# Layer 0 of a two-layer macaron block: attention work handed out one portion per score, FFN chains due later, and one FFN product moved to GpSimd

## The chip, the cores and the metric

One core of one Trainium2 chip runs the whole program in one launch. The metric is the device time of one execution in microseconds (us). The profile shows one execution: five engines with queues of their own (TensorE = PE for matmuls, PEld for its weight loads; VectorE = DVE; ScalarE = ACT; GpSimd = POOL; SyncE = SP, which here only issues DMAs). Each engine works through its own list of instructions strictly in order. That list is fixed when the program is built: a scheduler inside the tile framework takes the instructions in the order in which Python emits them as their priority, and places on each engine the first one that its own timing model holds ready. So the Python order is a wish, and the built order is what runs.

## The reference, cut to what matters

Sixteen sequences of 512 tokens with 128 features go through two layers. Layer 0 is FFN, attention, FFN:

```python
x = x + 0.5 * _L0_ffn_ref(_layernorm(x), w_gate, w_up, w_down)
x = x + _L0_attn_ref(_layernorm(x), W_qkv, b_qkv, W_out, b_out, rel_emb_k, rel_emb_v)
x = x + 0.5 * _L0_ffn_ref(_layernorm(x), w_gate, w_up, w_down)
# _L0_ffn_ref: every operand of a product is first quantised to FP4 in blocks of 16
gate = fp4_linear(x, w_gate); y = fp4_linear(x, w_up)
h = jax.nn.silu(gate) * y                     # 352 features
return fp4_linear(h, w_down)
# _L0_attn_ref: 16 heads of 8 features, relative positions clipped to +-64
score = einsum('bhqd,bhkd->bhqk', q, k) + einsum('bhqd,qkd->bhqk', q, pe_k)
attn = jax.nn.softmax(score, axis=-1)
ctx = einsum('bhqk,bhkd->bhqd', attn, v) + einsum('bhqk,qkd->bhqd', attn, pe_v)
```

Layer 1 (a mixture of experts, a linear attention, and the mixture again) is not touched by the change.

## The kernel before

**Units.** The attention of layer 0 is cut into 32 units: sequence b = 0..15 times half = 0, 1 (256 queries each). One unit needs 32 score tiles of 128 keys x 512 (four key tiles `kt` times eight query blocks `bb`), and it needs them twice. `maxima` computes each tile and VectorE reduces it to column maxima (line 341, tile `mx`); at the unit's end the maxima go through a transpose on TensorE (line 349), become a row `mn`, and are written to DRAM and back into a row of the query operand `BD`. `main` computes the tiles again, now with the maximum subtracted by the matmul, and ScalarE takes the exponential into `PT` (line 369). A score tile is four matmuls (line 263), and twelve where the block lies near the diagonal (the band: eight more, line 267). All score tiles of both kinds share three PSUM buffers (`sps`).

**Averages and band part.** After the eight tiles of one `kt`, `main` emits the 16 matmuls that average V (into `av`, two PSUM banks), and where a half-band is complete, two runs of matmuls for the relative values (into `rps`, one bank) and four ScalarE copies of it into `RV`. `run` (lines 270 to 274) chains the matmuls of one run. `PT` has three buffers. At the end of the unit `RV` goes to DRAM (`RD`) and back as `cr`, and ScalarE copies `av` to `cx`.

**Chains.** Around this run generators whose steps are emitted between the scores: `head` (the first FFN of a sequence's half), `prep` (layer norm, queries and keys, and the DMAs that write them to the DRAM tensors QS, QM and KSd), `prepV`, `fin` (adds `cr` to `cx` on VectorE, normalises, projects) and `tail` (the second FFN, then the store of x, line 486). `interleave` gives each generator a number of steps n and a stretch from f to t in units of time, and always advances the one whose next step is due first. `main` of unit u is due from u to u+1 with 59 steps; the stream of `maxima` runs from 0 to 32 and is 14 steps ahead.

**Loads.** In the middle of each unit's maxima `loads` brings in the operands of the unit after it: KS (keys, eight DMAs, once per sequence), BD (four, line 329) and TQ (four, line 330). `head` calls `xload` first, which loads the sequence's x into one of five buffers (line 475). All of these are issued from SP's queue.

**FFN.** `FFN.half` treats 256 tokens: layer norm, quantisation (`quant_steps`: VectorE, the last two steps on GpSimd, lines 79 and 81; tiles `q_y` and `q_M`, two buffers each), for each of two groups of 128 tokens the gate (lines 121 to 123) and the product with 'up' (lines 125 and 126), the quantisation of h, and the product with 'down'.

Of the kernel before, what the change touches and what calls it, by code (L numbers as in the profile page):

```python
# [8 lines left out]
F32 = mybir.dt.float32  # L9
# [3 lines left out]
AF = mybir.ActivationFunctionType  # L13
ALU = mybir.AluOpType
# [3 lines left out]
I = 352  # L18
# [65 lines left out]
class FFN:  # L84
# [22 lines left out]
    def half(f, xb, half, wk, pp):  # L107

        s=f.s; nc=s.nc
        xh=xb[:,2*half:2*half+2,:]  # L110
        xn=wk.tile([128,2,128],F32,name="f_x")
        yield from s.ln_steps(xh,xn,wk,2)
        for xq in s.quant_steps(xn.rearrange("p a b -> p (a b)"),wk,128,16,"xq"): yield
        ps=pp.tile([128,512],F32,name="mps")
        for j in range(2): nc.tensor.transpose(ps[:,j*128:(j+1)*128],xq[:,j*128:(j+1)*128],s.ident)
        xqT=wk.tile([128,256],F32,name="f_x"); nc.scalar.copy(xqT,ps[:,:256]); yield
        h=wk.tile([128,2,I],F32,name="f_h")
        for j in range(2):
            t=h[:,j,:]
            g=pp.tile([128,512],F32,name="mps")  # L120
            nc.tensor.matmul(g[:,:I],xqT[:,j*128:(j+1)*128],f.wguT[:,0,:],start=True,stop=True)
            nc.scalar.activation(t,g[:,:I],AF.Tanh,scale=0.5)
            nc.vector.scalar_tensor_tensor(t,t,1.0,g[:,:I],ALU.add,ALU.mult); yield
            u=pp.tile([128,512],F32,name="mps")
            nc.tensor.matmul(u[:,:I],xqT[:,j*128:(j+1)*128],f.wguT[:,1,:],start=True,stop=True)
            nc.vector.scalar_tensor_tensor(t,u[:,:I],0.5,t,ALU.mult,ALU.mult); yield
        for hq in s.quant_steps(h.rearrange("p a b -> p (a b)"),wk,128,44,"hq"): yield
        hq=hq.rearrange("p (a b) -> p a b",a=2)
        for j in range(2):
            ps=pp.tile([128,512],F32,name="mps")  # L130
            for c in range(3):
                P=min(128,I-c*128)
                nc.tensor.transpose(ps[:P,c*128:(c+1)*128],hq[:,j,c*128:c*128+P],s.ident)
            hT=wk.tile([128,3,128],F32,name="hT",bufs=1)
            nc.scalar.copy(hT[:,0:2,:],ps[:,:256])
            nc.scalar.copy(hT[:96,2,:],ps[:96,256:384])  # L136
            for c in range(3):
                P=min(128,I-c*128)
                nc.tensor.matmul(ps[:,384:512],hT[:P,c,:],f.wdT[:P,c,:],start=(c==0),stop=(c==2),skip_group_check=True)  # L139
            nc.vector.scalar_tensor_tensor(xh[:,j,:],ps[:,384:512],0.5,xh[:,j,:],ALU.mult,ALU.add); yield  # L140
# [5 lines left out]
class Attn0:  # L146
# [103 lines left out]
    @staticmethod  # L250
    def vers(kt,half):

        return 1 if kt*128+192<half*256+256 else 0
# [12 lines left out]
                w0=kt*128-blk*32-x+a.OFF  # L266
                nc.tensor.matmul(out[:,x*64:x*64+64],a.ET[:,w0:w0+128],TQ[:,:,b*32+4*x:b*32+4*x+4],start=False,stop=(x==7),skip_group_check=True)  # L267

    xnT={}; pend={}; last=None
    def run(a, mms):  # L270

        r=a.nc.tensor.matmul(*mms[0][0],**mms[0][1])
# [85 lines left out]
    def main(a, b, half, X, wk, big, pS, pA, pM):  # L358
        s=a.s; nc=a.nc; i=b%2
        u=(2*b+half)%3; BD=a.BD[u]; TQ=a.TQ[u]; KS=a.KS[b%2]; V=a.V[b%2]; RD=a.RD[half]; cr=a.cr[0]  # L360
        av=[pA.tile([128,512],F32,name=f"av{z}") for z in range(2)]
        RV=wk.tile([128,4,4,4,16],F32,name="RV")
        PT=[None]*4
        for kt in range(4):
            pt=big.tile([128,16,256],F32,name="PT"); PT[kt]=pt
            for bb in range(8):
                ps=pS.tile([128,512],F32,name="sps")
                a.scores(ps,kt,half,bb,BD,TQ,KS)
                nc.scalar.activation(pt[:,:,bb*32:bb*32+32].rearrange("p h (x j) -> p x h j",j=4),ps.rearrange("p (x h j) -> p x h j",x=8,j=4),AF.Exp)  # L369
                yield  # L370
            vs=a.vers(kt,half)
            mms=[]
            for z in range(4):
                for cg in range(4):
                    h=z*4+cg
                    o=av[z//2][cg*32:cg*32+32,(z%2)*256:(z%2)*256+256]
                    fs=(kt==0 and z%2==0)
                    mms.append(((o,V[:,2*kt-1+vs,h*9:h*9+32],pt[:,h,:]),dict(start=fs,stop=(kt==3),skip_group_check=True,tile_position=(0,cg*32))))
            a.run(mms)
            for _ in range(4): yield  # L380
            for hb in range(2):
                bl=range(hb*4,hb*4+4)
                ks=[k for k in range(4) if any(a.inband(k,half*8+x) for x in bl)]
                if max(ks)!=kt: continue
                rps=pA.tile([128,512],F32,name="rps")
                first=[True]*4
                mms=[]
                for b0 in bl[::2]:
                    ok=[(bb,k) for k in reversed(ks) for bb in (b0+1,b0) if a.inband(k,half*8+bb)]
                    for n,(bb,k) in enumerate(ok):  # L390
                        blk=half*8+bb
                        for x in range(8):
                            cg=x%4; col=(bb-hb*4)*128+(x//4)*64
                            v0=(blk*32-k*128+a.UO)//8
                            mms.append(((rps[cg*32:cg*32+32,col:col+64],a.TV[a.vers(k,half)][:,x,v0-8*a.vers(k,half):v0-8*a.vers(k,half)+4,:].rearrange("p v d -> p (v d)"),
                                PT[k][:,:,bb*32+4*x:bb*32+4*x+4]),
                                dict(start=first[cg],stop=(k==min(q for p,q in ok if p==bb)),skip_group_check=True,tile_position=(0,cg*32))))
                            first[cg]=False
                    a.run(mms); mms=[]
                    yield  # L400
                    yield
                for c in range(4):
                    nc.scalar.copy(RV[:,:,c,:,hb*8:hb*8+8].rearrange("p j z a -> p a z j"),rps.rearrange("p (a z c j) -> p c a z j",a=8,z=4,j=4)[:,c])
                yield

        nc.sync.dma_start(RD[:,:4*8*1024].rearrange("x (r f) -> x r f",f=1024),RV)
        for c in range(4):
            src=bass.AP(tensor=RD.tensor,offset=RD.offset+c*64,ap=[[1024,8],[8*1024+256,16],[1,64]])
            nc.sync.dma_start(cr[c*32:c*32+8].rearrange("p (xj f) -> p xj f",f=64),src)
        cx=wk.tile([128,4,256],F32,name="cx")  # L410
        for zz in range(2):
            nc.scalar.copy(cx[:,2*zz:2*zz+2,:].rearrange("p z (b j x) -> p (z b) x j",j=4,x=8),av[zz].rearrange("p (y x j) -> p y x j",x=8,j=4))
        a.pend[b,half]=cx,cr
        yield

    def fin(a, b, half, X, wk, pM):

# [28 lines left out]
def interleave(*gens):  # L446

    live=[[g,n,0,f,t] for g,n,f,t in (q if len(q)==4 else (*q,0,1) for q in gens)]
    while live:
        k=min(live,key=lambda r:r[3]+(r[4]-r[3])*r[2]/r[1])  # L450
        try: next(k[0]); k[2]+=1
        except StopIteration: live.remove(k)
# [4 lines left out]
def layer0(tc, s, w, src, dst, nb=16):  # L457
    nc=tc.nc
    tok=lambda x,b: x[b].rearrange("(t p) d -> p t d",p=128)
    P="L0_attn_"; names=["W_qkv","b_qkv","W_out","b_out","rel_emb_k","rel_emb_v"]  # L460
    with ExitStack() as c:
# [9 lines left out]
        X={}  # L471
# [7 lines left out]
        def prep(b):  # L479
            if b<nb: yield from A.prep(b,X[b],wk,pM)  # L480
        def prepV(b):
            if b<nb: yield from A.prepV(b,pM)
# [7 lines left out]
        def loads(u):  # L490
            if u<2*nb:
                if u%2==0: A.loadK(u//2)
                A.load(u//2,u%2)
# [6 lines left out]
        def part(n):  # L500
            for _ in range(n):
                if next(st,0)==0: return
                yield
        pl,hl=2,3
        W=dict(part=0,V=(.6,.7),fin=(.45,.9),prep=(0,.7),tail=1.0,head=(-.1,1))
        with tc.tile_pool(name="wp",bufs=1) as wp:
            for b in range(3): xload(b)
            F=FFN(s,w["L0_ffn_w_gate"],w["L0_ffn_w_up"],w["L0_ffn_w_down"],wp,pF)
# [3 lines left out]
            def run(g):  # L512
                for _ in g: pass
            run(prep(0)); run(prepV(0)); loads(0); run(mxs(0,0))
            FFN1.pre(s,wp,[pA.tile([128,512],F32,name=f"av{z}") for z in range(2)]+[pA.tile([128,512],F32,name="rps")],w)
        big=c.enter_context(tc.tile_pool(name="big",bufs=3))
        loads(1); ffn2(head,1); run(prep(1)); run(part(14)); ffn2(head,2)
        S=[(part(99999),33*2*nb,W['part'],2*nb+W['part'])]
        for b in range(nb):
            for h in range(2):  # L520
                u=2*b+h
                def at(g,n,f,t): S.append((g,n,u+f,u+t))
                at(A.main(b,h,X,wk,big,pS,pA,pM),59,0,1)
                fn,tl=(W['fin'],W['tail']) if u<2*nb-2 else ((.3,.5),.6)
                at(A.fin(b,h,X,wk,pM),5,1+fn[0],1+fn[1])
                at(tail(b,h),21,1+fn[1]+.001,1+fn[1]+tl)
                if b+hl<nb: at(head(b+hl,h),21,*W['head'])
                if h==0 and b+pl<nb: at(prep(b+pl),11,*W['prep'])
                if h==1 and b+1<nb: at(prepV(b+1),1,*W['V'])
        interleave(*S)  # L530


# [249 lines left out]
class Attn1:  # L782
# [38 lines left out]
    X={}  # L821
# [216 lines left out]
```

## Time and profile before

| what | value |
|---|---|
| time, median of 3 runs | 3639.21 us (3634.64 to 3644.63) |
| the profiled execution's own time | 3633.94 us |
| its span | 3632.2 us |
| busy over the span | PE 78%, DVE 67%, ACT 47%, POOL 23% |
| first and last exponential of layer 0 (line 369) | start 175.5 us, 1974.5 us |
| 422 to 1692 us (22 units, 11 sequences): PE busy | 1126.22 of 1270 us |
| the same stretch: DVE, ACT, POOL busy | 1013.48, 647.68, 306.91 us |
| the same stretch: granted clock of PE | 0.98 |

The units between 422 and 1692 us repeat each other in pairs, one pair per sequence, so one of them can be read as a sample of all. In that stretch TensorE is busy most and idle 143.8 us, so what it waits for there is what sets the time of layer 0. Idle time of the other engines costs nothing unless TensorE waits for them.

### The profile page before, as it was taken

Reading aid. Unit: us, or ns where it says so; the run is one execution under the profiler, and the core shown is the slowest. Engines: PE = TensorE matmul, PEld = TensorE weight load, DVE = VectorE, ACT = ScalarE, POOL = GpSimd, SP = SyncE. Lnnn points to the kernel's source line nnn. Section 1 sums busy time; section 2 is a strip of 40 time slices with the busy share of each in tenths; the row PEclk is TensorE's granted clock in tenths of the full one; section 3 lists DMA queues with packets and bytes.
Section 4 is the critical chain, followed back from the end, with each engine's and each line's share of the span. In section 5 each row is a group of like instructions: output and inputs, shape, how many; then the busy total and the mean of one; then the engine's idle time right before and its main releaser. Section 6 shows DMA issues by size and latency. Waiting matters only on the chain. (4 is left out here: it accounts for less than half of the span.)

```text
span 3632.2 us, 95259 instructions
## 1 busy us (share of the span) xinstructions
PE 2825.0 (78%) x40077; PEld 2032.3 (56%) x40077; DVE 2444.9 (67%) x6508; ACT 1693.8 (47%) x3391; POOL 838.9 (23%) x789
## 2 busy tenths in 40 slices
PE   5578989889898889888896388873788888878570
PEld 3357777667676677666775244431565555555230
DVE  5568788777887788877773467774546655655356
ACT  3145555545455454545554155533455454445242
POOL 4122222222222222222110222212112211111226
PEclk8799999999999999999998599886899989989785
DMA  3232222321223222222210111104312222121401
GB/s 105 54 91 71 57 53 59 81 63 52 65 65 77 64 50 58 76 74 62 53 33 19 32 33 36 36 33 123 90 54 73 59 63 56 36 62 36 126 17 46
DMA packets 290159, 217.23 MB, mean 60 GB/s; under 512 B 77402, under 2 KB 257476, under 8 KB 289604
## 3 DMA queue, kind: packets, MB, share of 16 engines
q1 hardware_dynamic: 284468, 207.72, 21.6%
q8 instruction: 315, 5.16, 0.6%
q10 hardware_dynamic: 5264, 3.43, 0.4%
q14 instruction: 112, 0.92, 0.1%
HBM read 110.28 MB, written 100.78 MB: 58 GB/s over the span
## 5 line engine op out<-in xcount | busy, mean ns | idle before, releaser
L341 DVE TRANSPOSE_TENSOR_REDUCE mx<-sps 128x16 f32<-128x512 f32 x1024 | 702.5, 701 | 261.7 <-PE sps L263 137.2
L263 PE MATMUL sps<-a_BD,a_KS 128*128 128x128 f16 x8192 | 736.4, 222 | 136.2 <-DVE mx L341 65.6
L369 ACT ACTIVATE PT<-sps 128x512 f32<-128x512 f32 x1024 | 576.4, 599 | 433.8 <-PE sps L267 238.1
L263 PEld LDWEIGHTS <-a_KS 128*128 128x128 f16 x8192 | 546.1, 98 | 296.4 <-issue 260.0
L59 POOL TENSOR_TENSOR ln_rs<-ln_ve,negh 128x4 f32<-128x4 f32 (+1 forms) x192 | 176.9, 930 | 855.1 <-DVE ln_ve L58 760.6
L267 PE MATMUL sps<-a_TQ,a_ET 128*128 128x64 f16 x7168 | 370.3, 195 | 0.0
L721 DVE SCALAR_TENSOR_TENSOR moe<-mps,oh,moe 128x128 f32<-128x128 f32 x896 | 289.8, 341 | 110.7 <-PE mps L719 96.5
L79 POOL TENSOR_TENSOR q_M<-q_y,q_M 128x704 f32<-128x704 f32 (+2 forms) x129 | 157.0, 1218 | 784.6 <-DVE q_y L78 658.6
L719 PE MATMUL mps<-f_W,T 128*128 128x512 f32 x512 | 297.1, 701 | 24.8 <-DVE moe L721 20.0
L267 PEld LDWEIGHTS <-a_ET 128*128 128x128 f16 x7168 | 311.2, 99 | 2.3 <-issue 1.9
L274 PE MATMUL av<-PT,a_V 128*32 128x256 f32 x3840 | 251.9, 387 | 0.0
L894 DVE TENSOR_TENSOR a_at<-pp,a_cm 128x1024 f32<-128x1024 f32 x128 | 154.3, 1214 | 79.6 <-PE pp L892 78.6
L892 PE MATMUL pp<-a_F 64*128 64x128 f32 x2048 | 169.8, 306 | 41.4 <-DVE a_at L894 30.2
L892 PEld LDWEIGHTS pp<-a_F 64*128 64x128 f32 x2048 | 143.3, 206 | 93.0 <-DVE a_at L894 36.9
L719 PEld LDWEIGHTS mps<-f_W,T 128*128 128x128 f32 x512 | 102.7, 222 | 125.0 <-issue 75.3
L274 PEld LDWEIGHTS av<-PT,a_V 128*32 128x32 f32 x3840 | 121.4, 111 | 68.7 <-issue 5.0
L874 ACT ACTIVATE a_F<-pp 128x1024 f32<-128x1024 f32 x128 | 127.0, 1025 | 46.8 <-PE pp L872 40.5
L62 ACT ACTIVATE xn<-xn,ln_mr,ln_rs 128x128 f32<-128x128 f32 x256 | 103.6, 481 | 95.5 <-DVE ln_mr L60 75.2
L274 PE MATMUL rps<-PT,a_TV 128*32 128x64 f32 x6912 | 134.5, 222 | 4.6 <-issue 4.4
L139 PE MATMUL mps<-wdT,hT 128*128 128x128 f32 (+1 forms) x768 | 126.9, 301 | 5.6 <-ACT hT L136 4.0
L673 ACT COPY f_PT<-St 32x512 f32<-32x512 f32 x128 | 78.7, 615 | 106.0 <-DVE St L672 99.9
L872 PE MATMUL pp<-a_QK,a_PK 128*128 128x512 f16 x256 | 82.7, 413 | 54.4 <-DMA a_QK<-a1d 26.6
(342 smaller groups left out, 5330.2 us busy)
## 6 DMA issues: line engine op xcount, KB each, us to landing
QM<-a_HM SPq DMA_DIRECT2D x180, 128.0 KB
a_TQ<-QM SPq DMA_DIRECT2D x120, 192.0 KB
RD<-RV SPq DMA_DIRECT2D x32, 512.0 KB
a_KS<-KSd SPq DMA_DIRECT2D x128, 96.0 KB
a_QK<-a1d SPq DMA_DIRECT2D x128, 96.0 KB
xn<-X SPq DMA_DIRECT2D x32, 256.0 KB
a1d<-a_hi SPq DMA_DIRECT2D x64, 128.0 KB
a_BD<-QS SPq DMA_DIRECT2D x128, 58.0 KB
```

What stands on the lines that cost most here:

```text
L59: nc.gpsimd.tensor_tensor(rs,ve,s.negh[:,:n],ALU.pow); yield
L79: nc.gpsimd.tensor_tensor(M[:P],y[:P],M[:P],ALU.subtract)
L263: nc.tensor.matmul(o4[:,g],KS[:,sd,g*512+kt*128:g*512+(kt+1)*128],BD[:,g,:,b*32:b*32+32].rearrange("p h (x j) -> p x h j",j=4),start=(g==0 ...
L267: nc.tensor.matmul(out[:,x*64:x*64+64],a.ET[:,w0:w0+128],TQ[:,:,b*32+4*x:b*32+4*x+4],start=False,stop=(x==7),skip_group_check=True)
L274: for p,q in mms[1:]: a.nc.tensor.matmul(*p,**q)
L341: with a.s.tc.high_priority(): r=nc.vector.tensor_reduce(mx[:,kt,:,bb],ps.rearrange("p (i c) -> p i c",c=32),axis=AX.X,op=ALU.max,apply_tr ...
L369: nc.scalar.activation(pt[:,:,bb*32:bb*32+32].rearrange("p h (x j) -> p x h j",j=4),ps.rearrange("p (x h j) -> p x h j",x=8,j=4),AF.Exp)
L719: nc.tensor.matmul(ps,yT[:,j*128:(j+1)*128],a.W[:,e2*4:e2*4+4,:],start=True,stop=True)
L721: nc.vector.scalar_tensor_tensor(moe[:,j,:],ps[:,e*128:(e+1)*128],oh[:,j,e2*4+e:e2*4+e+1],moe[:,j,:],ALU.mult,ALU.add)
L874: nc.scalar.activation(f,ps,AF.Relu)
L892: nc.tensor.matmul(ps[:,hh,bs],f[hh*64:hh*64+64,1,bs],f[hh*64:hh*64+64,0,bs],start=True,stop=True)
L894: nc.vector.tensor_tensor(k,ps.rearrange("p h (b q) -> p (h b) q",b=4),a.cm.unsqueeze(1).to_broadcast([128,8,128]),ALU.mult)
```

## The change

**Portions.** `main` no longer emits averages and band part itself. It appends them as closures to a list `a.todo`: one for the 16 averaging matmuls of a `kt` (`avrun`), one for each half of a half-band (`rvrun`), one for the four copies (`rvcopy`), and one for the unit's end (the write of `RD`, the reads of `cr`, the copies of `av`). After each score of `main` one closure is taken from the list and run. What is left at a unit's end is run after the scores of the next; `rest` empties the list after the last. `main` now has 32 steps where it had 59.

**Due times.** The prologue no longer calls `ffn2(head,2)`; `head` is called for the sequence two ahead instead of three (`hl` 3 to 2) and is due from -1.15 to -0.05 instead of -0.1 to 1, that is from 2b-5.15 instead of 2b-6.1 for half 0 of sequence b. `prep` is due from 1.0 to 1.9 instead of 0 to 0.7, `fin` from 0.6 to 1.0 instead of 0.45 to 0.9, and `tail` follows `fin` as before. `loads` stays where it was.

**The product with 'up'.** VectorE's instruction at line 126 (0.5 times the PSUM tile u, times t) becomes a ScalarE copy of u, scaled by 0.5, into a `q_y` buffer, and a GpSimd multiplication of t by it.

```diff
-            nc.vector.scalar_tensor_tensor(t,u[:,:I],0.5,t,ALU.mult,ALU.mult); yield
+            v=wk.tile([128,704],F32,name="q_y")[:,:I]; nc.scalar.activation(v,u[:,:I],AF.Copy,scale=0.5); nc.gpsimd.tensor_tensor(t,t,v,ALU.mult); yield
...
-        av=[pA.tile([128,512],F32,name=f"av{z}") for z in range(2)]
-        RV=wk.tile([128,4,4,4,16],F32,name="RV")
-        PT=[None]*4
+        PT=[None]*4; T={}; vers=a.vers
+        def avrun(kt):
+            if kt==0: T["av"]=[pA.tile([128,512],F32,name=f"av{z}") for z in range(2)]
...
+            a.run(mms)
+        def rvrun(hb, b0, ks):
+            if b0%4==0: T["rps"]=pA.tile([128,512],F32,name="rps"); T["first"]=[True]*4
...
+            a.run(mms)
+        def rvcopy(hb):
+            if hb==0: T["RV"]=wk.tile([128,4,4,4,16],F32,name="RV")
+            for c in range(4):
+                nc.scalar.copy(T["RV"][:,:,c,:,hb*8:hb*8+8].rearrange("p j z a -> p a z j"),T["rps"].rearrange("p (a z c j) -> p c a z j",a=8,z=4,j=4)[:,c])
+        def end():
...
         for kt in range(4):
             pt=big.tile([128,16,256],F32,name="PT"); PT[kt]=pt
             for bb in range(8):
                 ps=pS.tile([128,512],F32,name="sps")
                 a.scores(ps,kt,half,bb,BD,TQ,KS)
                 nc.scalar.activation(pt[:,:,bb*32:bb*32+32].rearrange("p h (x j) -> p x h j",j=4),ps.rearrange("p (x h j) -> p x h j",x=8,j=4),AF.Exp)
+                if a.todo: a.todo.pop(0)()
                 yield
-            vs=a.vers(kt,half)
-            mms=[]
...
-            a.run(mms)
-            for _ in range(4): yield
+            a.todo.append(lambda kt=kt: avrun(kt))
             for hb in range(2):
                 bl=range(hb*4,hb*4+4)
                 ks=[k for k in range(4) if any(a.inband(k,half*8+x) for x in bl)]
                 if max(ks)!=kt: continue
...
-                    a.run(mms); mms=[]
-                    yield
-                    yield
...
+                a.todo+=[lambda hb=hb,b0=b0,ks=ks: rvrun(hb,b0,ks) for b0 in bl[::2]]+[lambda hb=hb: rvcopy(hb)]
+            if kt==3: a.todo.append(end)
+    def rest(a):
+        while a.todo: a.todo.pop(0)(); yield
...
-        pl,hl=2,3
-        W=dict(part=0,V=(.6,.7),fin=(.45,.9),prep=(0,.7),tail=1.0,head=(-.1,1))
+        pl,hl=2,2
+        W=dict(part=0,V=(.6,.7),fin=(.6,1.0),prep=(1.0,1.9),tail=1.0,head=(-1.15,-.05))
...
-        loads(1); ffn2(head,1); run(prep(1)); run(part(14)); ffn2(head,2)
+        loads(1); ffn2(head,1); run(prep(1)); run(part(14))
...
-                def at(g,n,f,t): S.append((g,n,u+f,u+t))
-                at(A.main(b,h,X,wk,big,pS,pA,pM),59,0,1)
+                def at(g,n,f,t): S.append((g,n,max(u+f,0),max(u+t,.5)))
+                at(A.main(b,h,X,wk,big,pS,pA,pM),32,0,1)
...
+        S.append((A.rest(),8,2*nb,2*nb+.15))
         interleave(*S)
```

More of the change, by code (lines that the diff above doesn't have):

```diff
@@ L267, in scores @@
                 nc.tensor.matmul(out[:,x*64:x*64+64],a.ET[:,w0:w0+128],TQ[:,:,b*32+4*x:b*32+4*x+4],start=False,stop=(x==7),skip_group_check=True)
-    xnT={}; pend={}; last=None
+    xnT={}; pend={}; last=None; todo=[]
     def run(a, mms):
@@ L360, in main @@
         u=(2*b+half)%3; BD=a.BD[u]; TQ=a.TQ[u]; KS=a.KS[b%2]; V=a.V[b%2]; RD=a.RD[half]; cr=a.cr[0]
-        av=[pA.tile([128,512],F32,name=f"av{z}") for z in range(2)]
-        RV=wk.tile([128,4,4,4,16],F32,name="RV")
-        PT=[None]*4
+        PT=[None]*4; T={}; vers=a.vers
+        def avrun(kt):
+            if kt==0: T["av"]=[pA.tile([128,512],F32,name=f"av{z}") for z in range(2)]
+            vs=vers(kt,half)
+            mms=[]
+            for z in range(4):
+                for cg in range(4):
+                    h=z*4+cg
+                    o=T["av"][z//2][cg*32:cg*32+32,(z%2)*256:(z%2)*256+256]
+                    fs=(kt==0 and z%2==0)
+                    mms.append(((o,V[:,2*kt-1+vs,h*9:h*9+32],PT[kt][:,h,:]),dict(start=fs,stop=(kt==3),skip_group_check=True,tile_position=(0,cg*32))))
+            a.run(mms)
@@ new lines, in rvrun @@
+        def rvrun(hb, b0, ks):
+            if b0%4==0: T["rps"]=pA.tile([128,512],F32,name="rps"); T["first"]=[True]*4
+            rps=T["rps"]; first=T["first"]
+            mms=[]
+            ok=[(bb,k) for k in reversed(ks) for bb in (b0+1,b0) if a.inband(k,half*8+bb)]
+            for bb,k in ok:
+                blk=half*8+bb
+                for x in range(8):
+                    cg=x%4; col=(bb-hb*4)*128+(x//4)*64
+                    v0=(blk*32-k*128+a.UO)//8-8*vers(k,half)
+                    mms.append(((rps[cg*32:cg*32+32,col:col+64],a.TV[vers(k,half)][:,x,v0:v0+4,:].rearrange("p v d -> p (v d)"),
+                        PT[k][:,:,bb*32+4*x:bb*32+4*x+4]),
+                        dict(start=first[cg],stop=(k==min(q for p,q in ok if p==bb)),skip_group_check=True,tile_position=(0,cg*32))))
+                    first[cg]=False
+            a.run(mms)
@@ new lines, in rvcopy @@
+        def rvcopy(hb):
[3 more added lines that the diff above has]
+        def end():
+            nc.sync.dma_start(RD[:,:4*8*1024].rearrange("x (r f) -> x r f",f=1024),T["RV"])
+            for c in range(4):
+                src=bass.AP(tensor=RD.tensor,offset=RD.offset+c*64,ap=[[1024,8],[8*1024+256,16],[1,64]])
+                nc.sync.dma_start(cr[c*32:c*32+8].rearrange("p (xj f) -> p xj f",f=64),src)
+            cx=wk.tile([128,4,256],F32,name="cx")
+            for zz in range(2):
+                nc.scalar.copy(cx[:,2*zz:2*zz+2,:].rearrange("p z (b j x) -> p (z b) x j",j=4,x=8),T["av"][zz].rearrange("p (y x j) -> p y x j",x=8,j=4))
+            a.pend[b,half]=cx,cr
@@ L369, in main @@
                 nc.scalar.activation(pt[:,:,bb*32:bb*32+32].rearrange("p h (x j) -> p x h j",j=4),ps.rearrange("p (x h j) -> p x h j",x=8,j=4),AF.Exp)
+                if a.todo: a.todo.pop(0)()
                 yield
-            vs=a.vers(kt,half)
-            mms=[]
[L373 to L378, printed above, removed]
-            a.run(mms)
-            for _ in range(4): yield
+            a.todo.append(lambda kt=kt: avrun(kt))
             for hb in range(2):
@@ L384, in main @@
                 if max(ks)!=kt: continue
[L385 to L398, printed above, removed]
-                    a.run(mms); mms=[]
-                    yield
-                    yield
[L402 to L414, printed above, removed]
+                a.todo+=[lambda hb=hb,b0=b0,ks=ks: rvrun(hb,b0,ks) for b0 in bl[::2]]+[lambda hb=hb: rvcopy(hb)]
+            if kt==3: a.todo.append(end)
+    def rest(a):
+        while a.todo: a.todo.pop(0)(); yield
     def fin(a, b, half, X, wk, pM):
```

## The prediction, made before the changed kernel ran

> **What bounds the kernel.** I read first the busy times by window: between 422 and 1692 us (22 units, 11 sequences) TensorE is busy 1126 of 1270 us, VectorE 1013, ScalarE 648, GpSimd 307. Of an average unit of 57.7 us TensorE idles 6.5, so the question is what ends that idle time. Second, TensorE's waits there (engine, tile and line <- releaser: total us, times, longest):
>
> ```profile
> PE sps L263 <- DVE mx L341: 40.1, 45, 3.9
> PE sps L263 <- ACT PT L369: 21.6, 56, 0.8
> PE mps L437 <- DVE a_V L321: 19.2, 11, 1.8
> PE mps L440 <- ACT cn L438: 11.4, 9, 1.8
> PE sps L349 <- DVE hq_sc L71: 9.9, 11, 0.9
> PE sps L349 <- DVE mk L347: 5.2, 11, 0.5
> ```
>
> The first row means that scores wait for a score buffer which VectorE has not yet reduced. Why is VectorE late? Third view, VectorE's own waits:
>
> ```profile
> DVE ln_st L55 <- DMA x<-in_L_attn_x_dram: 41.1, 10, 5.2
> ```
>
> Once per sequence VectorE stands still for a load of x. Fourth, the timelines of SP, VectorE and TensorE around one such wait (start, us, instruction, [idle before <- releaser]):
>
> ```profile
> 873.37 0.39 SPq L486 DMA_DIRECT2D X<-x  x1
> 876.73 0.39 SPq L475 DMA_DIRECT2D x<-in_L_attn_x_dram  x1
> 877.21 1.68 SPq L315 DMA_DIRECT2D a_KS<-KSd  x4
> 878.93 0.26 SPq L329 DMA_DIRECT2D a_BD<-QS  x1
> ...
> 890.76 3.52 SPq L330 DMA_DIRECT2D a_TQ<-QM  x1
> 894.37 0.72 SPq L406 DMA_DIRECT2D RD<-RV  x1
> ```
> ```profile
> 879.93 1.07 DVE L55 BATCH_NORM_STATS2 ln_st<-x 128x6 f32<-128x128 f32 x5 [4.11 <-DMA x<-in_L_attn_x_dram]
> ```
> ```profile
> 882.54 0.39 PE L263 MATMUL sps<-a_BD,a_KS 128*128 128x128 f16 x4 [2.85 <-DVE mx L341]
> ```
>
> The tail's store frees the x buffer, SP issues the load, 3.2 us later (876.73 to 879.93) VectorE goes on, and the scores lose 4.11 - 1.26 = 2.85 us: the buffers in hand cover 1.26 us and no more. That difference is 1.26 to 1.28 in all eleven pairs of such waits; the ten TensorE gaps from 532 to 1573 us sum to 28.5 us, 2.87 each with the one at 415 us.
>
> **The change, part by part.** Fifth view: the built order of both kernels (what stands behind what on each engine; no times). Sums are for the whole layer, with 14 sequences and 28 units of this kind (28/22 of the stretch).
>
> (a) *The load of x*, moved by head's new due time. Eleven x loads (sequences 5 to 15) need a buffer that a tail frees. Before, SP's order is store, x load, rest of KS, eight BD and TQ loads, RD write. After: one KS, store, three KS, four pairs of BD and TQ, then the x load, then RD. VectorE's first `ln_st` of that x stays about five maxima further, with later maxima behind it, and scores wait for those. From the last score that frees KS: KS .42 + store .39 + KS 3 x .42 + BD and TQ 15.4 (878.93 to 894.37) = 17.5 us to the issue, plus 3.2 = 20.7. VectorE arrives when TensorE has done what lies between: three scores at .36 (four matmuls, 736.4/8192 = .090 each), five band scores at .77 (eight more at 370.3/7168), projections of the FFN 1.2, 16 averages 1.05 (251.9/3840), 16 band matmuls .3 (134.5/6912): 7.5 us, and .8 for the last reduction, 8.3. It waits 12.4 us, TensorE 11.1. ScalarE's burst there (two `cx`, four `RV`, a tanh, a copy: 5.2 us) should bring VectorE later by about one; I take 10.0. That is 10.0 - 2.87 = 7.1 more, x 11 = **+78 us**. Bounds: if the TQ pushes are as quick as where no KS load precedes (three in 1.33 us at 816.37), the wait is gone, 11 x -2.87 = -32; if ScalarE delays nothing and half the reads on SP take 1 us longer, +110.
>
> The clock follows the gaps:
>
> ```profile
> 884.00:888.00 4.00, 3.58 (x54) 3.46 (x52) 3.59 (x11) 2.81 (x8) 0.00 (x0) 0.57 0.23 62
> ```
>
> (0.57 is the granted clock.) In windows of 4 us just behind ten gaps the mean is 0.67, 1.3 us lost each; behind the 9.0 us gap at 246 us it is 0.50, 2.0 lost. So .7 x 11 = **+8** (-14 to +16). The Trainium skill, "TensorE: Matmul & The Clock Gate", section "Part 1: The HAM clock gate (the "warmup" mystery)", has the clock halve only after an idle window of some 3.4 us; by it gaps of 2.9 us would mostly cost nothing now and 10 us gaps 1.7 us each, an estimate of +19 instead of +8. The row, half clock behind a 2.85 us gap, speaks against that threshold here.
>
> (b) *Portions*: in the built order before, 260 pairs of main scores follow each other directly, and runs of three to nine maxima; after, the two kinds alternate. Waits for buffers are 40.1 + 21.6 - 28.5 (x) = 33.2, 42 for the layer. Between 0 and all of it: I take half, **-21**.
>
> (c) *`fin` spread out*: the rows of L437 and L440 (30.6, 39 for the layer) wait for links of a chain that was emitted in one burst; after, scores stand between the links. **-25** (-39 to 0).
>
> (d) *The maxima's transpose* (L349) waits .90 and .48 in turn. After, VectorE has more between a unit's last maximum and `mk`: in odd units two steps on 704 columns (.85, .98), two `mk` (.53 each), a maximum (.70), 3.6 us, against one band score and the band matmuls, 1.4 us, on TensorE; in even units 2.4 against .4. Wait about 2.1 instead of .7: 30 x 1.4 = **+42** (0 to +60).
>
> (e) *Averages directly behind a key tile's last score* wait for the exponential (.60). One score of the next tile and usually a maximum lie between: **+5** (0 to +25).
>
> (f) *The product*:
>
> ```profile
> L126 DVE SCALAR_TENSOR_TENSOR f_h<-mps,f_h 128x352 f32<-128x352 f32 x88 | 44.1, 501 | 0.0
> L122 ACT ACTIVATE f_h<-mps 128x352 f32<-128x352 f32 x89 | 42.2, 474 | 30.7 <-PE mps L121 29.8
> L79 POOL TENSOR_TENSOR q_M<-q_y,q_M 128x704 f32<-128x704 f32 x44 | 73.9, 1681 | 408.8 <-DVE q_y L78 369.3 <-PE sps L263 31.6 <-issue 7.9
> L79 POOL TENSOR_TENSOR q_M<-q_y,q_M 128x256 f32<-128x256 f32 x45 | 32.7, 726 | 101.5 <-DVE q_y L78 98.6 <-PE sps L263 1.5 <-DMA a_BD<-QS 1.4
> ```
>
> 128 instructions: VectorE -.50 each, -64 us; ScalarE +.38 (L116's copy, 128x256) to +.47 (L122), +58; GpSimd, between the two L79 rows, .93 each, +119. None sets the end: ScalarE is 51% busy and GpSimd 24%, and VectorE's freed time is idle time unless it is late. The copy waits for a `q_y` buffer and holds ScalarE's later exponentials behind it; `hq_sc` waits for the product, with maxima behind it. The built order keeps at least four maxima (2.8 us) between product and `hq_sc`, more than .45 + .93. I take **0**; VectorE's relief could give -10, and without that cover .93 x 64 = +60. The Trainium skill, "SBUF — State Buffer", section "Who interferes with whom", speaks against this part: GpSimd and a VectorE operation with two SBUF inputs exclude each other from a shared port, the second blocked wholly. By that rule up to 128 x .93 = 119 us of VectorE's work would be blocked, an estimate in place of 0. No row here prices it; `ln_ve`, a small VectorE step, varies from 103 to 1104 ns and may be it.
>
> (g) Prologue: an FFN half goes from ahead of the first exponential into the stream, while the built order ahead of it keeps nearly the same content: **0** (±5).
>
> Sum: 78 + 8 - 21 - 25 + 42 + 5 = +87. On the profiled execution's own 3633.9 that is 3721; the median stands 5.3 above it: **3726**.
>
> **The rivals.**
> R1, *faster*: the x load is not late. SP's slow pushes are those of units that also load KS; if they go fast behind the new order, the load leaves at about +8 us, and that is the point from which it decides: below it VectorE never waits. For: 816.37. Against: the four TQ pushes at 882 to 894. Then -32 for x, and clock 0: -32 - 21 - 25 + 42 + 5 = -31, to -45 with the clock's -14: about 3600 (3590 to 3625).
> R2, *same*: every term at a mild end, x and clock +55, d +20, b -42, c -39: -6, 3633. For: b and c are chains of plain waits that the new order does break. Against: x needs a queue a third faster than the one seen.
> R3, *slower still*: the product arrives late at `hq_sc` because its copy stands in ScalarE's queue behind the burst of `cx` and `RV`; VectorE loses .93 x 64 = 60 more: 3786. It decides once copy and product need over 2.8 us. For: `cx` is 1.08 us, two in a row. Against: four maxima of cover.
> That the scheduler ignores the portions is no rival: the built order shows them one per score.
>
> **How the numbers follow.** Forecast .62 (own range 3670 to 3770), R1 .18, R2 .08, R3 .12. About 0.3%, 11 us, is what a measurement of this kernel can tell from no change. Faster .19 (R1 and the low edge of R2), same .06, slower .75. The range 3625 to 3790 leaves out most of R1 and the upper half of R3.
>
> **What would show it.** Right: SP's order has L475 behind the last L330, issued some 17 us behind KS; VectorE waits about 12 us for x, eleven times; TensorE has one gap of about 10 us per sequence, the clock near 0.5 behind it; L349 waits about 2 us; L437 and L440 leave the list of waits; line 126 appears on ScalarE near 450 ns and on GpSimd near 930. Wrong: x waits under 3 us (R1), or waits at `hq_sc` for GpSimd (R3); or if a gap starves nothing because TensorE finds averages and band runs to do meanwhile, which the built order hardly offers.

## The result, and the profile after

The changed kernel takes 3839.61 us (median of 4 runs, 3836.23 to 3842.89); the kernel before, in the same comparison, 3636.93 us. The ratio is 1.056, 95% interval 1.0529 to 1.059: some 203 us slower. The forecast was slower, at 3726 us and at most 3790. The sign was right, and so was the place of the largest loss, the late load of x; the predicted loss of 87 us fell far short of the 203 that came.

TensorE's waits of the changed kernel between 422 and 1692 us, the stretch that was shown of before (9.5 sequences here, 11 there; releaser: total us, times, longest):

```profile
PE sps L263 <- DVE mx L341: 148.8, 33, 14.9
PE sps L349 <- DVE mk L347: 52.4, 19, 3.6
PE mps L434 <- DVE mn L352: 17.3, 9, 2.1
PE sps L263 <- ACT PT L407: 16.3, 43, 0.7
PE sps L263 <- DVE mt L351: 13.0, 9, 1.6
```

The first row has grown from 40.1 to 148.8 us, with a longest wait of 14.9. As before, the score buffers are late because VectorE stands still for x. VectorE's own list, the timelines of SP, VectorE and TensorE around one such wait:

```profile
DVE ln_st L55 <- DMA x<-in_L_attn_x_dram: 148.0, 10, 15.4
```
```profile
1077.03 0.29 SPq L315 DMA_DIRECT2D a_KS<-KSd  x1
1077.42 0.38 SPq L490 DMA_DIRECT2D X<-x  x1
1077.85 1.27 SPq L315 DMA_DIRECT2D a_KS<-KSd  x3
1079.16 0.26 SPq L329 DMA_DIRECT2D a_BD<-QS  x1
...
1090.84 3.48 SPq L330 DMA_DIRECT2D a_TQ<-QM  x1
1094.36 0.74 SPq L479 DMA_DIRECT2D x<-in_L_attn_x_dram  x1
1095.20 1.04 SPq L394 DMA_DIRECT2D RD<-RV  x1
1105.77 0.27 SPq L397 DMA_DIRECT2D a_cr<-RD  x1
```
```profile
1100.35 0.48 DVE L55 BATCH_NORM_STATS2 ln_st<-x 128x6 f32<-128x128 f32 x2 [15.16 <-DMA x<-in_L_attn_x_dram]
```
```profile
1101.93 0.58 PE L263 MATMUL sps<-a_BD,a_KS 128*128 128x128 f16 x4 [14.64 <-DVE mx L341]
```

The load of x leaves 17.3 us after the first KS push, behind four pairs of BD and TQ, and VectorE goes on 6.0 us after that. The clock pays too. In windows of one sequence (us, length, busy time of PE, PEld, DVE, ACT, POOL, granted clock, DMA share, GB/s):

```profile
1102.00:1106.00 4.00, 4.00 (x24) 2.81 (x24) 2.03 (x4) 1.20 (x3) 0.04 (x1) 0.50 0.18 67
1106.00:1110.00 4.00, 4.00 (x61) 2.69 (x58) 1.84 (x3) 2.54 (x5) 0.94 (x1) 0.93 0.15 33
1128.00:1132.00 4.00, 3.00 (x32) 2.58 (x30) 3.68 (x6) 2.39 (x4) 3.77 (x2) 0.69 0.02 6
1188.00:1192.00 4.00, 4.00 (x35) 2.66 (x32) 3.67 (x6) 0.64 (x2) 1.55 (x1) 0.51 0.25 35
```

The clock is 0.50 behind the x gap, and again 0.69 and 0.51 behind the waits at the maxima's transpose (L349), one in each unit. Over the stretch from 422 to 1692 us the granted clock is 0.89; it was 0.98.

A sequence (two units) now takes 133.2 us instead of 115.5, averaged over ten of them: TensorE is idle 28.0 us of it (13.1 before) and busy 105.2 (102.4). The last exponential of layer 0 comes at 2191 us instead of 1975, 216 us later; the rest of the span is 13 us shorter.

### The profile page after: what moved, and what is told of

The parts are those of the page before. It is cut to its first block, busy times and chain, and to the rows that moved or that the text cites. A ratio compares the mean times of both kernels' runs of the same rounds, so it can differ in the third digit from the quotient of the medians.

```text
span 3835.6 us, 95480 instructions
## 1 busy us (share of the span) xinstructions
PE 2851.4 (74%) x40077; PEld 2075.9 (54%) x40077; DVE 2439.8 (64%) x6380; ACT 1763.4 (46%) x3519; POOL 980.5 (26%) x917
## 5 line engine op out<-in xcount | busy, mean ns | idle before, releaser
L407 ACT ACTIVATE PT<-sps 128x512 f32<-128x512 f32 x1024 | 598.2, 600 | 840.9 <-PE sps L267 549.8
L263 PE MATMUL sps<-a_BD,a_KS 128*128 128x128 f16 x8192 | 757.8, 228 | 280.2 <-DVE mx L341 182.0
L263 PEld LDWEIGHTS <-a_KS 128*128 128x128 f16 x8192 | 572.1, 101 | 451.8 <-issue 422.3
L267 PE MATMUL sps<-a_TQ,a_ET 128*128 128x64 f16 x7168 | 383.2, 198 | 0.0
L267 PEld LDWEIGHTS <-a_ET 128*128 128x128 f16 x7168 | 324.3, 102 | 2.0 <-issue 1.8
L79 POOL TENSOR_TENSOR q_M<-q_y,q_M 128x704 f32<-128x704 f32 (+2 forms) x129 | 163.7, 1270 | 386.9 <-DVE q_y L78 284.4
L126 POOL TENSOR_TENSOR f_h<-f_h,q_y 128x352 f32<-128x352 f32 x128 | 124.2, 974 | 459.2 <-ACT q_y L126 331.0
L55 DVE BATCH_NORM_STATS2 ln_st<-x 128x6 f32<-128x128 f32 x192 | 48.3, 279 | 164.5 <-DMA x<-in_L_attn_x_dram 163.3
L121 PE MATMUL mps<-wguT,f_x 128*128 128x352 f32 x256 | 116.5, 560 | 19.8 <-ACT f_x L116 19.1
```

What stands on the lines that cost most here:

```text
L79: nc.gpsimd.tensor_tensor(M[:P],y[:P],M[:P],ALU.subtract)
L263: nc.tensor.matmul(o4[:,g],KS[:,sd,g*512+kt*128:g*512+(kt+1)*128],BD[:,g,:,b*32:b*32+32].rearrange("p h (x j) -> p x h j",j=4),start=(g==0 ...
```

## The experiments

Eighteen kernels ran. Any edit lets the scheduler place other instructions anew, so an experiment changes more than its line; each reading below rests on the waits in that kernel's own trace. Times are medians; the kernel before stood between 3639 and 3646 us beside them.

### The x load, and each part alone

**e1.** The changed kernel, with

```diff
-            nc.sync.dma_start(t,tok(src,b))
+            with tc.high_priority(): nc.sync.dma_start(t,tok(src,b))
```

> The changed kernel with one edit: the load of x (line 479) is issued at high priority, which puts it on SP's queue straight behind the four KS loads instead of behind the four pairs of BD and TQ. Theory A (the x load stuck behind BD and TQ is most of the loss): the load leaves when the store has landed, about 14 us earlier, VectorE's wait of 14.8 us and TensorE's gap of 14.2 us go in eleven places: -156 us, and some 1.5 us of half clock each, -16: about 3670 us. Rival B (the time is set by stalls in the middle of a sequence and by the clock, the freed time is given back there): no more than -60, about 3780. Rival C (the transfer itself is late whatever the order, since BD and TQ fill the DMA engines): the wait shrinks by under 5 us, about 3785.

Measured: 3749.18 us, ratio 1.0299 (1.0276 to 1.0323). VectorE's wait for x fell from 148.0 to 15.2 us. That is 90 us of the 203 for one DMA's place in a queue, between the 60 of rival B and the 170 of theory A: something else took a part back. It is in TensorE's waits for ScalarE's exponentials, which grew from 16.3 to

```profile
PE sps L263 <- ACT PT L407: 66.4, 49, 5.9
```

In ScalarE's own list a row of 58.3 us is new, for the copies into `RV` that wait until RD is written; e9 below takes it up.

**e2, e3, e4.** The kernel before with one part of the change each: due times, product, portions.

> The kernel before with the due times alone (hl 2, fin, prep and head as in the change; no second FFN head ahead of the stream). Averages, band part and product stay. SP's order puts store and x load behind BD and TQ, but the layer norm that reads x is some four scores later still. Theory A: the x wait stays near 3 us, so the due times alone cost little through x; about 3640 to 3680. Rival B (due times gather VectorE's steps around the maxima's transpose and fin): L349 waits of 2 to 3.6 us and half clock behind them, 3700 to 3760.

> The kernel before with the product alone on ScalarE and GpSimd. The built order also moves the x load behind two or three pairs of BD and TQ pushes. Theory A: the wait for x grows from 4 to 6 to 10 us, 11 times: 3660 to 3710, and the product itself adds nothing. Rival D (GpSimd's product blocks VectorE, up to 0.9 us a product): VectorE's steps on SBUF get longer, and 60 us or more come on top, 3720 or more. If neither, within 10 us of before.

> The kernel before with the portions alone (averages and band part one per score, main with 32 steps, old due times, old product). SP's order has the x load straight behind the store, before the last KS loads, and the layer norm just behind it. Theory A: the x wait is 4 to 6 us, nearly as before, and the alternation of scores and maxima saves up to 20 us: 3600 to 3650. Rival B (portions leave VectorE late at the transpose of the maxima): waits of 2 us at L349, +30 to +60, 3670 to 3700.

Measured: due times alone 3872.36 us (ratio 1.0632, 1.0602 to 1.0663), product alone 3745.29 (1.028, 1.0256 to 1.0305), portions alone 3689.46 (1.0134, 1.0115 to 1.0154). Every part costs, and together (203 us) they cost less than their sum (230, 103 and 47 us), so at least some of them share a cause. VectorE's waits name it for e2 and, below it, for e3:

```profile
DVE ln_st L55 <- DMA x<-in_L_attn_x_dram: 209.1, 10, 22.1
```
```profile
DVE ln_st L55 <- DMA x<-in_L_attn_x_dram: 94.2, 11, 9.2
```

The time of e3 lies in the range of its rival D, although its x wait (94.2 / 11 = 8.6 us each) is what theory A had; what the product costs by itself is read from e13 and e16 below. My expectation for e2 was wrong: I had counted SP's pushes, not what SP itself waits for. Its timeline in e2 shows that:

```profile
1103.44 3.48 SPq L330 DMA_DIRECT2D a_TQ<-QM  x1
1107.01 0.71 SPq L406 DMA_DIRECT2D RD<-RV  x1
1116.43 1.36 SPq L409 DMA_DIRECT2D a_cr<-RD  x4
1117.89 0.39 SPq L486 DMA_DIRECT2D X<-x  x1
1120.54 0.39 SPq L475 DMA_DIRECT2D x<-in_L_attn_x_dram  x1
```

SP stands from 1107.7 to 1116.4 us, because the read of `cr` waits until the write of RD has landed, and store and load of x are queued behind that read. So a DMA that waits holds what stands behind it in SP's list, as an instruction does on an engine. e4 has little x wait (31.0 us); there VectorE waits for another DMA, in line 307, before it writes `qklo`:

```profile
DVE qklo L307 <- DMA QS<-qkhi: 49.4, 11, 5.4
```

### x on another queue

**e5 to e8.** Store and load of x leave SP for GpSimd's queue, in four kernels: due times alone, and the changed kernel without portions, without the product, without the due times.

```diff
-            nc.sync.dma_start(t,tok(src,b))
+            (nc.gpsimd if b>2 else nc.sync).dma_start(t,tok(src,b))
...
-            nc.sync.dma_start(tok(dst,b)[:,2*h:2*h+2,:],X[b][:,2*h:2*h+2,:])
+            nc.gpsimd.dma_start(tok(dst,b)[:,2*h:2*h+2,:],X[b][:,2*h:2*h+2,:])
```

> The kernel before with the due times alone, as in e2, and the store (line 486) and the load of x (line 475, from the fourth sequence on) issued from GpSimd's queue, so that they stand behind no BD, TQ or KS push. Theory A (in e2 the 20 us gap per sequence is the place of store and load in SP's queue, and nothing else of the due times costs): the wait of VectorE falls from 20.9 to under 5 us, 11 times, and the half clock behind it: 3620 to 3670. Rival B (the due times cost through the transpose of the maxima): 3690 or more.

> The changed kernel without the portions (due times and product stay), store and load of x on GpSimd's queue. If the parts add up once x is out of the way (due and product near 0, portions +47 as in e4): about 3640 to 3670. If due times and product are worse together than alone (GpSimd's work and VectorE's steps meet at the transpose of the maxima): 3700 or more.

> The changed kernel without the product's move (portions and due times stay), store and load of x on GpSimd's queue. If the parts add up: portions' +47, about 3680 to 3700. If the rest of e1's +107 comes from GpSimd's work getting in VectorE's way: 3650 to 3690. If it comes from portions and due times together: 3730 to 3750.

> The changed kernel with the old due times (portions and product stay), store and load of x on GpSimd's queue. If the parts add up: about 3680 to 3700, as e4, with the wait for qklo at line 307 as there. If the rest of e1's +107 needs the new due times: below 3700; if it needs only portions and product: 3730 to 3750.

Measured: e5 3719.97 us (ratio 1.0218, 1.0178 to 1.0258), e6 3788.34 (1.0404, 1.0371 to 1.0437), e7 3726.06 (1.0229, 1.0195 to 1.0263), e8 3686.8 (1.0128, 1.0088 to 1.0167). e5 lost 152 us of e2's 230, so the queue was most of it, but x stayed late; its time lies in rival B's range, and does not speak for B, since the wait that was to go is still there (84.8 us). GpSimd's timeline in e5 (VectorE's instruction last):

```profile
1034.74 0.77 POOL L486 DMA_DIRECT2D X<-x  x1 [2.59 <-DVE x L140]
1040.90 0.81 POOL L475 DMA_DIRECT2D x<-in_L_attn_x_dram  x1 [3.91 <-DMA X<-x]
1049.69 0.48 DVE L55 BATCH_NORM_STATS2 ln_st<-x 128x6 f32<-128x128 f32 x2 [9.37 <-DMA x<-in_L_attn_x_dram]
```

Even with nothing ahead of them in their queue, the chain from store over load to layer norm is 15 us long here, and where the new due times call `head` less than that after the tail that frees its buffer, VectorE waits. The load alone takes 8.8 us from issue to use, against 3.2 in the kernel before; SP's last TQ load (issued at 1036.17 us) and the write of RD (1039.75) go out just ahead of it, but no run shows that they are what slows it. e6 and e7 keep such waits (79 and 80 us), so the four do not separate the parts; they were inconclusive for that. e8, with the old due times, came where it was expected (3680 to 3700, as e4); it has 23 us of x waits and instead e4's wait at line 307 (52.9 us on TensorE). The load has to leave earlier, not only by another queue.

### x loaded by halves, right behind the store

**e9 to e12.** x gets five fixed tiles, and `tail` loads each half of the next sequence into its place as soon as its own half is stored:

```diff
+            if b>4: X[b]=X[b-5]; return
...
             nc.sync.dma_start(tok(dst,b)[:,2*h:2*h+2,:],X[b][:,2*h:2*h+2,:])
+            if b+5<nb: nc.sync.dma_start(X[b][:,2*h:2*h+2,:],tok(src,b+5)[:,2*h:2*h+2,:])
```

> The changed kernel with x in five fixed tiles, and each half of the next x loaded by tail right behind its own store (half 0 a unit earlier than before). No layer norm then follows its load by less than some 24 scores. Theory A: no wait for x in VectorE's list at all; what stays above the kernel before is what the change costs without the load: about 3740, as e1 (whose x waits sum to 15 us). If e8's and e5's costs were mostly the store-to-load chain: 3640 to 3700. Rival C (loads too slow whatever the order): waits of over 5 us stay, 3800.

> The kernel before with the half loads of e9. Theory A: its eleven x gaps (31.6 us) and the half clock behind them (up to 14) go: 3595 to 3612. If the freed time is given back at another wait: 3625 to 3640.

> The kernel before with the due times alone and half loads. Theory A: the due times cost nothing but the x wait: within 20 us of e10, 3590 to 3630. If they cost by themselves (waits of 2 us at the maxima's transpose, line 349, half clock behind): 3650 to 3690.

> The kernel before with the product alone and half loads. Theory A: the product costs nothing but the x wait that its order brings: within 15 us of e10, 3590 to 3625. Rival D (GpSimd's product and VectorE's steps with two SBUF operands block each other): 3650 to 3720.

Measured: e9 (the changed kernel) 3726.95 us, ratio 1.0238 (1.0199 to 1.0278); e11 (due times alone) 3645.6, 1.0009 (0.9988 to 1.003); e10 (kernel before) 3763.61, 1.0333 (1.0287 to 1.0379); e12 (product alone) 3879.78, 1.066 (1.0622 to 1.0698).

e9 and e11 have no wait for x at all. With that wait gone, the new due times are level with the kernel before (e11, against +230 in e2). Theory A had wanted 3590 to 3630, because the kernel before's own x gaps (31.6 us) are gone in e11 too; about as much has come up elsewhere, most of it in the waits for `mx`: 56.5 us here, and 40.1 before, of which 28.5 were x. e10 and e12 missed badly: they keep the old due times, which call `head` three sequences ahead, and there the tail that frees a buffer ends just before `head` wants it, now in both halves. In the timeline of e10 such a half load also stands behind SP's read of `cr`, which waits for RD, as in e2: the store goes out at 1132.69 us, the read at 1142.00, the load at 1143.10. e10 has twenty x waits instead of ten:

```profile
DVE ln_st L55 <- DMA x<-in_L_attn_x_dram: 132.8, 20, 9.6
```

So which parts are harmless can't be read off e10 and e12. What e9 keeps, 84 us, is the second part of the loss. ScalarE's waits in e9, and one of them in its timeline:

```profile
ACT RV L391 <- DMA RD<-RV: 67.5, 11, 7.2
```
```profile
1054.61 0.60 ACT L407 ACTIVATE PT<-sps 128x512 f32<-128x512 f32 x1 [0.15 <-PE sps L267]
1061.09 1.01 ACT L391 COPY RV<-rps 128x128 f32<-128x128 f32 x4 [5.88 <-DMA RD<-RV]
1061.91 1.10 ACT L407 ACTIVATE PT<-sps 128x512 f32<-128x512 f32 x2
```

The copies into `RV` wait until its only buffer has been written to DRAM, with the exponentials behind them, and the write stands on SP behind the same TQ pushes that delayed x (the last one starts at 1048.00 us, RD goes out at 1051.90 and its read follows at 1061.03).

### RD on ScalarE's own queue, and the parts left out

**e13 to e16.** e13 is e9 with

```diff
-            nc.sync.dma_start(RD[:,:4*8*1024].rearrange("x (r f) -> x r f",f=1024),T["RV"])
+            nc.scalar.dma_start(RD[:,:4*8*1024].rearrange("x (r f) -> x r f",f=1024),T["RV"])
```

e14 is e9 without the product, e15 e9 without the portions, e16 e14 with RD as in e13.

> e9 with the write of RD (line 394) issued from ScalarE's queue instead of SP's, where it stands behind the last TQ push. In e9 the next copies into RV wait 67.5 us for that write (11 times, longest 7.2), and scores lose 4 to 6 us behind them. Theory A (RD behind BD and TQ is the second victim of SP's queue): these waits go, -50 to -60 and some 10 of clock, 3655 to 3680. Rival B (the maxima's transpose takes it back): 3700 to 3730.

> The changed kernel without the product's move, with the half loads of e9 (no x wait). If what e9 keeps (+84) comes from portions and due times: 3710 to 3730. If it needs the product: 3640 to 3680.

> The changed kernel without the portions (due times and product), with half loads. If the rest comes from the portions (RD written late, steps of VectorE ahead of the maxima's transpose): 3640 to 3660, near e11. If due times and product alone cost: 3690 or more.

> e14 with the write of RD from ScalarE's queue. By Theory A both victims of SP's queue are out and VectorE and GpSimd do not meet in the product: 3610 to 3660; with the waits at the transpose as in e9 (45 us in 1270): 3660 to 3690.

Measured: e13 3655.4 us, ratio 1.0027 (1.0007 to 1.0047); e14 3727.98, 1.0217 (1.0183 to 1.0252); e15 3687.75, 1.0102 (1.0066 to 1.0138); e16 3646.82, 1.0006 (0.9985 to 1.0028).

e13 is the whole change with nothing of its computing undone, only with x loaded ahead of BD and TQ and RD written from ScalarE's queue, and it is 10 us from the kernel before by the ratio (16 by the medians). In its trace no computing engine waits for x in this stretch, and none for the write of RD; only SP does, for its read of `cr`. e14 says that the product was not the cause (it even kept 91.9 us of RD waits), and from e14 to e16 the step of RD is there a second time: 81 us, after 72 from e9 to e13. e15 says that RD is late because of the portions: without them that wait is 8.4 us. e13 and e16 differ by the product alone and stand 8.6 us apart, and their intervals overlap.

Two things stay open. e15 has neither of the two waits and still stands 48 us above the kernel before, between its two expectations, at a clock of 0.93; what costs it that is not shown, so the parts do not add up even without x and RD. And the kernel before has x gaps of its own, 31.6 us in all, which e13 does not have; e10, which was to take them out there, failed. So e13 shows that the loss goes with the two DMAs, and not that the rest of the change is free.

What e13 has left:

```profile
PE sps L263 <- ACT PT L407: 43.6, 86, 2.0
PE sps L349 <- DVE mk L347: 40.0, 22, 2.0
PE sps L263 <- DVE mx L341: 28.9, 27, 2.3
PE sps L263 <- DVE mt L351: 16.1, 11, 1.6
```

### The maxima's transpose

**e17, e18.** e13, with two and three steps of the stream between VectorE's `mk` and the transpose, so that scores of `main` cover the wait (the stream's count of steps goes from 33 to 35 and 36):

```diff
             nc.vector.tensor_reduce(mk[:,hh],mx.rearrange("p k (x s) b -> p s b x k",s=2)[:,hh],axis=AX.X,op=ALU.max)
+        for _ in range(2): yield
```

> e13 with the transpose of the maxima (line 349 there, now 350) emitted two steps of the stream later, so that two scores of main stand on TensorE between VectorE's last maximum and the transpose. e13's waits for mk are 40 us in 22 units (51 for the layer) and for mt 16 (20). If they set the time: mk's waits fall to under 10 us, -40 to -60 with some clock, 3595 to 3620, faster than the kernel before. If the freed time goes to another wait (score buffers): 3640 to 3660.

> As e17 with three steps; the built order then also puts the tail's store in the middle of a unit, away from the KS, BD and TQ pushes. If waits for mk and mt set the time: 3590 to 3620. If not: 3640 to 3660.

Measured: e17 3638.95 us, ratio 0.9989 (0.9976 to 1.0001); e18 3873.62, 1.0629 (1.0612 to 1.0647). In e17 the rows for mk and mt, 56 us in e13, are gone, and most of it came back in another row, up from 28.9:

```profile
PE sps L263 <- DVE mx L341: 75.6, 55, 3.2
```

e17 is level with the kernel before; no version that ran is clearly faster than that. e18 has the same edit with one step more, and a built order in which VectorE comes to `fin`'s adds 13 us behind ScalarE's copies of `cx` (ready at 985.53, copies from 972.70), where e13 has 37. In both the read of `cr` stands behind BD and TQ pushes on SP, one of which takes 8.68 us in e18; in e13 it goes out 17 us before the adds (1021.34 and 1038.88), in e18 VectorE stands still for it, with four maxima behind:

```profile
987.55 3.54 SPq L330 DMA_DIRECT2D a_TQ<-QM  x1
991.20 2.32 SPq L398 DMA_DIRECT2D a_cr<-RD  x4
```
```profile
997.38 2.13 DVE L427 TENSOR_TENSOR cx<-cx,a_cr 128x512 f32<-128x512 f32 x2 [11.85 <-DMA a_cr<-RD]
999.42 2.74 DVE L341 TRANSPOSE_TENSOR_REDUCE mx<-sps 128x16 f32<-128x512 f32 x4
```

## Why the prediction had the main path right and the sum wrong

The path through the load of x, VectorE and the scores came as predicted. What failed is the sum: x was 48 us too small, the clock 32 and the transpose 15, the gains of (b) and (c) were 33 too large, and waits of some 30 us stood in no term. By the prediction's own terms, each worked out from the changed kernel's waits in ten sequences (414.4 to 1746.4 us), per sequence, times 14 (11 for x):

| term | predicted | measured | how |
|---|---|---|---|
| (a) x on TensorE | +78 | +126 | gap 14.29 instead of 2.87 us, x 11 |
| clock, as busy time of TensorE | +8 | +40 | 105.2 - 102.4 = 2.8 x 14 |
| (b) alternation | -21 | -9 | 2.35 against 3.02 x 14 |
| (c) `fin` | -25 | -4 | 2.5 against 2.8 x 14 |
| (d) transpose, mk | +42 | +57 | 5.43 against 1.37 x 14 |
| wait for `mt`, not listed | 0 | +20 | 1.45 x 14 |
| (e) averages | +5 | 0 | no row |
| band run's wait for the exponential (L272), not listed | 0 | +10 | 0.69 x 14 |
| small waits that went or shrank, not listed | 0 | -23 | 1.18 against 2.85 x 14 |

These give 217, against 216 us that layer 0 grew. What the product (f) costs is inside these rows; e13 against e16 puts it at about +9, where 0 was taken.

**(a) The x load.** SP's order, the 17.5 us to the issue (17.3 measured) and VectorE's arrival 8.3 us after the first push (1085.19, that is 8.2) were right. Wrong was the landing: I took 3.2 us from a load that stood ahead of BD and TQ, and behind them it is 6.0 (1094.36 to 1100.35). Wrong too were the cover of TensorE (1.26 us taken, 0.5 found) and the microsecond for ScalarE's burst, which did not delay VectorE. Together the gap was 4.3 us longer than the 10.0 taken, in eleven places.

**The clock.** I priced it behind the x gaps alone. The clock is down behind the waits at the transpose as well: 0.69 in the window behind one of 3.60 us (ending at 1127.07), 0.51 behind three of 0.69, 1.90 and 1.57 us in six microseconds (1180 to 1186). Each of them had to carry a clock term of its own.

**(b) and (c), the gains.** They came to 13 us of the 46 claimed. The waits at `fin`'s later links did go (L437 and L440 of before), as predicted, but TensorE now waits at the first link, L434, for VectorE's adds of `cr` to `cx`, twelve times in ten sequences. One of them, on GpSimd, VectorE and TensorE:

```profile
1128.15 1.73 POOL L79 TENSOR_TENSOR q_M<-q_y,q_M 128x704 f32<-128x704 f32 x1 [0.89 <-DVE q_y L78]
1129.50 3.55 DVE L426 TENSOR_TENSOR cx<-cx,a_cr 128x512 f32<-128x512 f32 x2
1129.96 2.12 POOL L81 TENSOR_TENSOR q_M<-q_M,hq_sc 128x704 f32<-128x704 f32 x1
1133.11 1.30 PE L434 MATMUL mps<-ident,cx 128*128 128x128 f32 x8 [1.81 <-DVE mn L352]
```

The two adds take 3.55 us beside GpSimd's quantisation (L79, L81), and TensorE waits until they and the short `mn` behind them are done; a pair that runs alone takes 2.09 us. Of the twenty pairs of these sequences twelve run beside L79 and L81 (2.6 to 4.4 us a pair), and each of the twelve waits at L434 (1.5 to 3.0 us) stands behind one of them; behind the other eight there is none. In the kernel before no pair of the stretch from 422 to 1692 us meets these steps. So most of the gain was taken back by something that the prediction had put at nothing, GpSimd in VectorE's way; it had looked for it at the product alone. In e13 no pair is slowed (1.09 us an add in the mean, 1.69 in e9), and the waits at L434 are 3.8 us, after 27.9 in e9: a part of e13's 72 us came by this, and not by RD. e14 and e16, 81 us apart, have adds of 1.10 and 1.12 us in the mean. No run changes this alone.

**(d)** was a third low per wait (2.1 us predicted, 52.4/19 = 2.8 found), and the wait for `mt` just behind it was missed. But e17 shows what such a wait is worth once others are ready to take its place: 56 us of waits removed brought 16 (14 by the ratios).

**What the prediction did not see.** It named the RD write in SP's order, behind the x load, and did not ask who waits for it. In the changed kernel itself no row shows that wait, and it appears as soon as x is earlier (58.3 us in e1, 67.5 in e9); that the stop for x had given RD its time is the likely reason. The steps from 3839.6 over e9 (3727.0) and e13 (3655.4) to e17 (3639.0) are therefore an order of removal and not separate prices: x 113, RD 72, the transposes 16. RD alone was not tried with x late. What e13 shows is that 184 of the 203 us go when both DMAs are moved.

**The rivals.** R1 and R2 (x not late) fell with the first timeline. R3 (VectorE waits at `hq_sc` for GpSimd's product) has no row in the changed kernel's list of VectorE's waits. In e8 and e12, with the old due times, there is such a row, of 13.1 and 11.6 us. The estimate of up to 119 us for the product, worked out from the Trainium skill, "SBUF — State Buffer", section "Who interferes with whom", was not borne out in the time: the product cost about 9. The interference as such shows in the rows above: `cx` (L426) takes 3.55 us for two while GpSimd runs L79 and L81 beside it, 1.10 each in the mean before.

## What to carry to other kernels

When a change moves work in a single DMA queue, write down that queue's order before and after, and for every transfer that lands further back ask which engine holds its next instruction for it: here x (VectorE), RD (ScalarE), `cr` (VectorE) each stopped an in-order engine with the scores behind it. In this kernel a read that waited for a write to land held up the rest of SP's list (e2), and it paid to issue that write from the queue of the engine that made its data (e13, e16). A load directly behind the store that frees its buffer helped where it came well ahead of its use (e9, e11), and made things worse where it did not (e10, e12). A wait that is in no list may stand right behind the largest one: price a repair by running it, not by adding up rows.

## What had not been expected of the hardware

The push of one TQ load of 192 KB takes SP 0.44 us where no KS load goes ahead (three in 1.33 us at 816.37 us of the kernel before), and 3.3 to 3.5 us as second to fourth of a row behind KS (from 1082.20 us in the changed kernel; once 8.68 in e18). The load of x, 256 KB, needs 3.2 us from issue to use ahead of that row, 6.0 behind it, and 8.8 from GpSimd's queue in e5. After a write of RD, 512 KB, its read starts 9 to 11 us later (9.4 at 1107.01 us in e2, 10.6 at 1095.20 in the changed kernel). Two adds of `cx` take 2.09 us on VectorE, and up to 4.4 us beside GpSimd's quantisation steps.
